# Four graph attention layers from packed neighbour lists: lists split by upper and lower half of the target rows

## The chip, the cores and the metric

The kernel runs on one core of one Trainium2 chip. The metric is the device time of one execution in microseconds (us). A core has TensorE (PE, with its weight loads shown as PEld), VectorE (DVE), ScalarE (ACT), GpSimd (POOL), SyncE (SP) and 16 DMA engines. The profile shows one execution.

## The reference

Four layers work on one graph of 4096 nodes with 256 features. Each is `x = layernorm(x + gat(x, adj))`. The adjacency has one entry in 256, plus the diagonal, and is the same in all layers. Layers 0 and 1 have four heads of 64 columns, layer 2 has two heads of 128, and layer 3 has one score with a positive and a negative softmax, each of 256 columns. Cut to what matters:

```
h = (x @ W.T).reshape(C, H, D).transpose(1, 0, 2)
e = alpha_src[:, :, None] + alpha_dst[:, None, :]
e = leaky_relu(e, 0.2); e = where(adj == 0, -inf, e)
out = einsum('hij,hjd->hid', softmax(e, axis=-1), h)
```

Layer 3 takes `softmax(e)` and `-softmax(-e)`, multiplies both by `x`, joins them, multiplies by `fc_W` and applies elu.

## The kernel before

**Tiles.** Target nodes are worked on in 32 row tiles of 128 (`P`). A row tile needs only the source nodes that touch any of its 128 targets, some 40% of them. So the kernel builds, once, a list for each row tile: the source nodes outside the tile that have an entry in it, packed into 13 tiles of 128 (`NG`), with an 8-bit mask of 128 targets for each listed node. The row tile's own 128 nodes are a fourteenth tile at position 6 (`FRONT`). All four layers use the same lists. Where a list doesn't fit its windows, a flag is set and `dense_layers` computes everything again at the end.

**Lists** (`Program.lists`). A block of four row tiles is read by `prepare`: 67 MB of adjacency in all arrive as int32, ACT turns them into bytes (L385) and DVE finds which source nodes touch which tile (L389). `places` (L394) ranks the hits with a few small matmuls and about nine DVE operations. `pack` (L427) then goes through the 31 other source blocks of a row tile: a DVE comparison makes a one-hot matrix of the places that this block can reach (L440, 128 to 384 columns by `WINDOW`), and one matmul for each reachable tile (L446, 73 for a row tile) moves mask bytes and the node number's digits to their place, 132 columns (`MC`). ACT copies three packed tiles at a time out of PSUM (L453), in five copies for a row tile, and DVE puts the digits together to the index list (L460 to L462). The packing banks come in turn from three PSUM banks (`pthree`).

**Order.** `run` computes layer 0's projections first, with the first ten packs and the `prepare` parts between them (`LEAD = 10`). Then it goes through layer 0's row tiles, and between the two halves of each of the first 22 it builds one more list. A scheduler orders the instructions of each engine from there; each engine works through its own queue in order.

**A row tile** (`RowTile`). It has two halves of seven positions (`HALF`). `load` (L632) loads the scores `S`, the masks `mk`, and one row of values for each listed node: a direct DMA on SP for the tile's own rows (L644) and an indirect one on POOL for each of the 13 other positions (L647). The first six of them reach only the first 17 blocks of nodes (`MIX`), so they can start before the layer before has stored the rest. The rows land in buffers `G` of two pools, `g0` with 16 and `g1` with 14, two positions in a buffer, in layer 3 one. `half` (L651) makes the weights `w`, 128 listed nodes by 128 targets for each position and head: in layers 0 and 1 ACT takes three heads' exponentials (L712) and DVE one head's product (L704, L708), then DVE masks two heads at a time (L681), after it has copied the masks to PSUM (L666). In layer 2 ACT does both heads and DVE masks each (L714); in layer 3 it is L690 to L694. TensorE multiplies them. In layers 0 and 1 the values are the stationary operand, 65 columns, and the weights stream (L724); the result stands transposed, so `copy` (L749) and `back` (L757) turn it round. In layers 2 and 3 the weights are stationary and the values stream, 129 and 257 columns (L727). `finish` normalises, adds the residual, and `norm` applies the layer norm to groups of tiles; `Projection` then makes the next layer's rows.

**Whole rows.** In layer 2 the blocks 3, 7 and 6, and in layer 3 the block 7, are not taken from lists: `whole_rows` goes over all 32 source blocks with four row tiles at a time (L1016 to L1027). These steps are spread between the list tiles (20 in layer 2, 28 in layer 3). At a layer's end `close` projects what is left and already loads and computes first halves of the next layer.


Of the kernel before, what the change touches and what calls it, by code (L numbers as in the profile page):

```python
# [50 lines left out]
P = 128  # L51
# [19 lines left out]
NG = 13  # L71
NP = NG + 1
CAP = NG * P
HALF = NP // 2

GROUPS = (((24, 4),), ((28, 2),), ((16, 2), (17, 1), (20, 2), (24, 1), (31, 2)), ((28, 1), (31, 4)))
LEAD = 10
MIX = 17
FRONT = 6
NODES = tuple(MIX * P if t < FRONT else N for t in range(NG))  # L80
MC = P + 4
# [11 lines left out]
KEXP = 10.0  # L93

# [11 lines left out]
def windows():  # L106

    share = 1.0 - (1.0 - 1.0 / 256.0) ** P
    mean, sd = P * share, (P * share * (1.0 - share)) ** 0.5
    dev = 4.5  # L110
    out = {}
    for m in range(NT):
        for j in range(NT):
            if j == m:
                continue
            if j < MIX:
                n = sum(q != m for q in range(j))
                lo = mean * n - dev * sd * n ** 0.5
                hi = mean * (n + 1) + dev * sd * (n + 1) ** 0.5
            else:  # L120
                n = sum(q != m for q in range(j, NT))
                lo = CAP - mean * n - dev * sd * n ** 0.5
                hi = CAP - mean * (n - 1) + dev * sd * (n - 1) ** 0.5
            a = max(0, int(lo // P))
            b = min(NG - 1, int((hi - 1) // P))
            out[m, j] = (a, b - a + 1)
    return out
# [3 lines left out]
assert all(a >= FRONT for (m, j), (a, _) in WINDOW.items() if j >= MIX)  # L131
WMAX = max(n for _, n in WINDOW.values()) * P
# [7 lines left out]
def kernel(ctx: ExitStack, tc: tile.TileContext, ins: dict, out: bass.AP):  # L140
# [14 lines left out]
        "maskC": dram.tile([NT, P, NP, MC], U8, name="maskC"),  # L155
# [38 lines left out]
class Program:  # L194


    def __init__(self, tc, ctx, ins, out, shared):
# [5 lines left out]
        self.g0 = self.pool("g0", 16)  # L203
# [89 lines left out]
    def lists(self, ctx):  # L293
# [21 lines left out]
        for k, sh in enumerate((8, 4, 0)):  # L315
# [21 lines left out]
        nc.gpsimd.affine_select(out=bt[:, :, :MIX], in_=bt[:, :, :MIX], pattern=[[NT, BT], [1, MIX]],  # L337
                                compare_op=ALU.is_gt, fill=0.0, base=0, channel_multiplier=-1)
        nc.vector.tensor_scalar(bt[:, :, MIX:], bt[:, :, MIX:], -1.0, None, op0=ALU.mult)

        nc.gpsimd.affine_select(out=bt[:, :, MIX:], in_=bt[:, :, MIX:], pattern=[[-NT, BT], [-1, NT - MIX]],
                                compare_op=ALU.is_ge, fill=0.0, base=-MIX, channel_multiplier=1)


        lo = cst.tile([P, NT, NT], F16, name="lo")
        wid = cst.tile([P, NT, NT], F16, name="wid")
        nc.gpsimd.memset(lo, 0.0)
        nc.gpsimd.memset(wid, 0.0)
        for j in range(NT):
            m = 0  # L350
            while m < NT:
                if m == j:
                    m += 1
                    continue
                e = m
                while e < NT and e != j and WINDOW[e, j] == WINDOW[m, j]:
                    e += 1
                a, n = WINDOW[m, j]
                nc.gpsimd.memset(lo[:, m:e, j], a * P - 1.0 - (CAP if j >= MIX else 0))
                nc.gpsimd.memset(wid[:, m:e, j], float(n * P))  # L360
                m = e
        limit = cst.tile([P, NP], F32, name="limit")
        nc.vector.memset(limit[:, :FRONT], float(MIX * P - 1))
        nc.vector.memset(limit[:, FRONT:], float(N - 1))
        total = cst.tile([P, NT], F32, name="total")
        bad = cst.tile([P, BT, NT], F32, name="bad")
        nc.vector.memset(bad, 0.0)

        class Block:
            def __init__(self, blk):  # L370
                self.blk = blk
                self.mk = mkp.tile([P, NT, BT, MC], U8, name="mk")
                self.red = wk.tile([P, BT, NT], F32, name="red")
# [53 lines left out]
            def pack(self, it):  # L427
# [4 lines left out]
                for j in order:  # L432
                    a, n = WINDOW[m, j]
                    for k in range(a, a + n):
                        touches.setdefault(k // 3, []).append((j, k))
# [1154 lines left out]
```

## Time and profile before

| | |
|---|---|
| three runs | 2753.11 us median (2740.87 to 2766.65) |
| span of the profiled execution, first to last instruction | 2249.3 us |
| mean granted TensorE clock in it | 0.966 |
| busy in the span | PE 2014.0, DVE 1786.6, ACT 1737.9, POOL 1494.4 us |
| gathers (L647) | 1456, mean 1017 ns busy |
| DMA | 493 MB, mean 219 GB/s |
| chain that ended last | PE 16% of the span, of it L727 12% and L1027 4% |

The profile gives no time for the profiled execution but its span; what lies around the span is seen only as the difference to the runs. In the profile's rows a group is named by its line, engine and operation, then output and inputs, then the count, busy time and mean duration. Starts are counted from the span's start. Busy time on PE is modelled, and matmuls overlap, so the distance between starts tells more than a duration. Layer 0's first half tile starts on PE at 168 us, layer 1 follows at about 810, layer 2 at 1340, and layer 3 at 1757.

### The profile page before, as it was taken

To read this page: it belongs to the slowest core of one execution; us is meant where nothing else is said; L and a number is where in the kernel's file an instruction comes from. 1 tells how busy PE (TensorE), PEld (TensorE's weight loads), DVE (VectorE), ACT (ScalarE), POOL (GpSimd) and SP (SyncE) were. 2 spreads that over 40 slices of the span, in tenths; PEclk is the share of its full clock that TensorE was granted. 3 is DMA by queue.
4 is the path that set the end of the run, shared out by engine and by line. 5 is a ranking of instruction groups with operands and counts; after the bars stand their busy time and mean duration, and the time that the engine had idled before them with its cause. 6 is when DMAs were issued, how large, how long until landed. Compare 5 with 4: busy or idle time off the path is not lost. (4 is left out here: it accounts for less than half of the span.)

```text
span 2249.3 us, 49137 instructions
## 1 busy us (share of the span) xinstructions
PE 2014.0 (90%) x15689; PEld 1834.3 (82%) x15689; DVE 1786.6 (79%) x5060; ACT 1737.9 (77%) x4989; POOL 1494.4 (66%) x1597
## 2 busy tenths in 40 slices
PE   4878889989999969988899898989999999999995
PEld 2658788878899859988888798989998888788784
DVE  2889899999999959987988886887876566566566
ACT  4778988988789859987888776987876677667664
POOL 2107655656677777777777777777773477777773
PEclk7999999999999989999999999999999999999998
DMA  8879877777566665666665666777777688888884
GB/s 284 258 245 360 272 219 250 254 247 228 146 170 191 174 202 168 182 175 175 173 185 162 172 167 171 226 209 223 223 227 225 200 282 280 249 284 270 262 248 130
DMA packets 250319, 492.99 MB, mean 219 GB/s; under 512 B 44385, under 2 KB 156610, under 8 KB 249666
## 3 DMA queue, kind: packets, MB, share of 16 engines
q0 software_dynamic: 81536, 245.30, 38.3%
q1 hardware_dynamic: 163906, 240.26, 33.3%
q10 hardware_dynamic: 4608, 4.20, 0.5%
q8 instruction: 126, 2.06, 0.4%
q14 instruction: 143, 1.17, 0.2%
HBM read 437.05 MB, written 52.54 MB: 218 GB/s over the span
## 5 line engine op out<-in xcount | busy, mean ns | idle before, releaser
L647 POOL DMA_INDIRECT G<-vals,idx x1456 | 1480.7, 1017 | 715.7 <-issue 221.1
L712 ACT ACTIVATE w<-S,G 128x128 f32<-128x128 f32 x3248 | 1001.6, 390 | 140.6 <-DMA G<-vals,idx 101.6
L724 PE MATMUL bank<-w,G 128*65 128x128 f32 x7168 | 837.8, 276 | 59.7 <-DVE w L681 59.3
L724 PEld LDWEIGHTS bank<-w,G 128*65 128x65 f32 x7168 | 798.7, 140 | 69.9 <-DVE w L681 68.4
L681 DVE SCALAR_TENSOR_TENSOR w<-w,bank 128x1792 f32<-128x1792 f32 x256 | 514.6, 2013 | 13.4 <-ACT w L712 11.2
L727 PE MATMUL bank<-G,w 128*128 128x257 f32 (+1 forms) x2660 | 490.8, 342 | 25.7 <-ACT z L1102 13.6
L727 PEld LDWEIGHTS bank<-G,w 128*128 128x128 f32 x2660 | 431.9, 195 | 73.2 <-ACT z L1102 16.4
L1027 PE MATMUL bank<-vw,pw 128*128 128x129 f32 (+1 forms) x2048 | 298.5, 301 | 3.7 <-issue 2.3
L1027 PEld LDWEIGHTS bank<-vw,pw 128*128 128x128 f32 x2048 | 273.6, 191 | 20.1 <-issue 2.8
L690 ACT ACTIVATE w<-S,G 128x128 f32<-128x128 f32 x385 | 137.8, 393 | 136.8 <-DMA G<-vals,idx 90.0
L440 DVE TENSOR_SCALAR oh<-iota,place 128x256 bf16<-128x256 f16 (+2 forms) x992 | 221.8, 298 | 9.4 <-PE bank L446 9.1
L704 DVE TENSOR_TENSOR w<-S,G 128x256 f32<-128x256 f32 x384 | 151.9, 416 | 69.9 <-DMA G<-vals,idx 66.5
L446 PE MATMUL bank<-mk,oh 128*128 128x132 fp8e4 x2336 | 192.1, 226 | 13.8 <-ACT cm L453 7.0
L557 PE MATMUL bank<-wext,xT 128*128 128x268 f32 (+3 forms) x640 | 176.9, 409 | 16.9 <-ACT xT L548 14.1
L446 PEld LDWEIGHTS <-oh 128*128 128x128 bf16 x2336 | 146.9, 99 | 50.4 <-DVE oh L440 12.7
L385 ACT ACTIVATE mk<-raw 128x1024 uint8<-128x1024 int32 x128 | 130.5, 1051 | 28.0 <-DMA raw<-in_adjB_dram 27.7
L557 PEld LDWEIGHTS bank<-wext,xT 128*128 128x128 f32 x640 | 117.2, 200 | 36.0 <-ACT xT L548 16.9
L1017 DVE SCALAR_TENSOR_TENSOR pw<-pw,mw 128x512 f32<-128x512 f32 x192 | 127.6, 689 | 18.2 <-ACT pw L1016 17.5
L1016 ACT ACTIVATE pw<-Sw,d 128x512 f32<-128x512 f32 x192 | 133.2, 711 | 7.5 <-PE bank L1027 7.0
L714 DVE SCALAR_TENSOR_TENSOR w<-w,mk 128x896 f32<-128x896 f32 x80 | 86.6, 1086 | 41.1 <-ACT w L712 37.9
L1024 DVE TENSOR_TENSOR pw<-pw,mw 128x512 f32<-128x512 f32 x64 | 43.6, 691 | 85.4 <-ACT pw L1023 48.0
L692 DVE TENSOR_TENSOR w<-w,mk 128x896 f32<-128x896 f32 x55 | 60.0, 1091 | 59.5 <-ACT w L691 58.2
(140 smaller groups left out, 1563.3 us busy)
## 6 DMA issues: line engine op xcount, KB each, us to landing
raw<-in_adjB_dram SPq DMA_DIRECT2D x128, 512.0 KB
mk<-maskC SPq DMA_DIRECT2D x112, 231.0 KB
G<-vals,idx POOLq DMA_INDIRECT x1456
S<-edge SPq DMA_DIRECT2D x64, 256.0 KB
vw<-vals SPq DMA_DIRECT2D x96, 129.0 KB
xp<-y SPq DMA_DIRECT2D x96, 128.0 KB
y<-xp SPq DMA_DIRECT2D x96, 128.0 KB
mw<-maskW SPq DMA_DIRECT2D x20, 528.0 KB
```

Of the source, the lines that this page charges most:

```text
L440: nc.vector.tensor_scalar(oh[:, :n * P], iota[:, :n * P], self.place[:, it, j:j + 1], None, op0=ALU.is_equal)
L446: nc.tensor.matmul(accs[b][:, s * MC:(s + 1) * MC], oh[:, (k - a) * P:(k - a + 1) * P], mk[:, j, it, :].bitcast(FP8), start=touches[b][0] ...
L557: nc.tensor.matmul(pp[:, :c1 - c0], self.xT[:, k, :], wext[:, k, c0:c1], start=(k == 0), stop=(k == KT - 1 and brow is None))
L647: nc.gpsimd.indirect_dma_start(out=self.place(pos), out_offset=None, in_=sh["v"][n][:NODES[t], :], in_offset=bass.IndirectOffsetOnAxis(ap= ...
L681: nc.vector.scalar_tensor_tensor(pair, pair, LEAST, mh2, op0=ALU.max, op1=ALU.mult)
L690: nc.scalar.activation(w[0][:, k, :], S[:, 0, :], AF.Relu, bias=d(k, 0))
L704: nc.vector.tensor_tensor(w[h][:, k:k + 2, :], S[:, h:h + 1, :].to_broadcast([P, 2, P]), dd[:, :, V + T + h:V + T + h + 1].to_broadcast([P ...
L712: nc.scalar.activation(w[h][:, k, :], S[:, h, :], AF.Exp, bias=d(k, h))
L724: nc.tensor.matmul(accs[0][:Wd, h * P:(h + 1) * P], v, w[h][:, k, :], **how)
L727: nc.tensor.matmul(a, w[h][:, k, :], v, **how)
L1016: nc.scalar.activation(p, S[:, h], AF.Exp, bias=d)
L1027: nc.tensor.matmul(accs[it][:, c:c + Wd], p[:, it, :], v[:, c:c + Wd], start=(j == 0 and h == heads[0]), stop=(j == NT - 1), skip_group_ch ...
```

## The change

The targets of a row tile are split into its upper and lower 64 rows. A source node that touches only one half of the rows is put into a list for that half, one that touches both is put into a mixed list. Five packed tiles hold the upper list and five the lower one; they are taken in pairs, and a pair shares one block of weights of 128 columns, the first 64 for the upper gather and the last 64 for the lower. Three mixed tiles hold the nodes that touch both halves and what the five-tile lists can't take. With the tile's own rows there are nine blocks of weights (`NU`) in place of fourteen, from the same thirteen indirect gathers and one direct load. The first half of a row tile has four blocks (its own, three pairs), the second five (two pairs, three mixed).

With it: `lists` ranks three classes, keeps one window for each class and source block, and writes the node's digits twice; `MIX` goes from 17 to 23; a buffer `G` holds seven positions (in layer 3 four), with four buffers in each of `g0` and `g1`; in all layers the weights are now the stationary operand, 64 columns wide for the members of a pair, with the output in the upper or lower 64 PSUM partitions; `copy` and `back` are gone. The core of the diff:

```diff
-NG = 13
-NP = NG + 1
-CAP = NG * P
-HALF = NP // 2
+HP = P // 2
+NPAIR = 5
+NMIX = 3
+NPACK = NPAIR + NMIX
+NU = NPACK + 1
+NP = 2 * NPAIR + NMIX
+HALF = 7
+FIRST = 3
+UNITS = (1 + FIRST, NPACK - FIRST)
+FULL = ((0,), tuple(range(NPAIR - FIRST, NPACK - FIRST)))
+PAIRS = (tuple(range(1, 1 + FIRST)), tuple(range(NPAIR - FIRST)))
...
-MIX = 17
-FRONT = 6
-NODES = tuple(MIX * P if t < FRONT else N for t in range(NG))
-MC = P + 4
+MIX = 23
+MC = P + 8
...
+PER = tuple(HALF if n < 3 else 4 for n in range(4))
+SLOT = max(p * r for p, r in zip(PER, ROW))
...
-        self.g0 = self.pool("g0", 16)
+        self.g0 = self.pool("g0", 4)
...
-        self.g1 = self.pool("g1", 14)
+        self.g1 = self.pool("g1", 4)
...
             def places(self):
...
+                cls = wk.tile([P, 3, BT, NT], BF16, name="cls")
+                nc.vector.tensor_scalar(cls[:, :2], self.red, 0.0, None, op0=ALU.is_gt)
...
+                nc.vector.tensor_tensor(flat[:, 2], flat[:, 0], flat[:, 1], op=ALU.mult)
+                nc.vector.tensor_tensor(flat[:, 1], flat[:, 1], flat[:, 2], op=ALU.subtract)
...
+                nc.vector.scalar_tensor_tensor(far, at[:, :2], float(NPAIR * P), cls[:, :2], op0=ALU.is_ge,
+                                               op1=ALU.mult)
...
+                nc.vector.tensor_tensor(place, place, here[:, 0], op=ALU.add)
+                nc.vector.tensor_tensor(place, place, here[:, 1], op=ALU.add)
...
             def pack(self, it):
...
-                    nc.vector.tensor_scalar(oh[:, :n * P], iota[:, :n * P], self.place[:, it, j:j + 1], None,
-                                            op0=ALU.is_equal)
-                    for k in range(a, a + n):
+                    nc.vector.tensor_scalar(oh[:, :len(ks) * P], iota[:, :len(ks) * P], self.place[:, it, j:j + 1],
+                                            None, op0=ALU.is_equal)
+                    for i, k in enumerate(ks):
...
-    def place(self, pos):
+    def slot(self, half, s):
         L, n = self.layer, self.layer.n
-        per = 1 if n == 3 else 2
-        s = pos // per
-        if s not in self.slots:
-            if n == 3:
-                other = self.step % 2 == 0 if self.step > 3 else self.step > 1 and s < HALF
-            else:
-                other = n > 0 and s * per >= HALF
-            pool = L.prog.g1 if other else L.prog.g0
-            self.slots[s] = pool.tile([P, 2 * ROW[0]], F32, name="G")
+        if (half, s) not in self.slots:
+            pool = L.prog.g1 if n > 0 and half else L.prog.g0
+            self.slots[half, s] = pool.tile([P, SLOT], F32, name="G")
+        return self.slots[half, s]
...
+            nc.sync.dma_start(out=self.place(0, 0), in_=sh["v"][n][m * P:(m + 1) * P, :])
...
+        for k in range(1 - half, HALF):
+            pos = half * HALF + k - 1
             nc.gpsimd.indirect_dma_start(
-                out=self.place(pos), out_offset=None, in_=sh["v"][n][:NODES[t], :],
+                out=self.place(half, k), out_offset=None, in_=sh["v"][n][:N if half else MIX * P, :],
                 in_offset=bass.IndirectOffsetOnAxis(ap=sh["idx"][:, m, pos:pos + 1], axis=0))
+    def parts(self, half):
+        out, k = {}, 0
+        for u in range(UNITS[half]):
+            if u in PAIRS[half]:
+                out[u] = [(slice(0, HP), self.place(half, k)), (slice(HP, P), self.place(half, k + 1))]
+                k += 2
+            else:
+                out[u] = [(slice(0, P), self.place(half, k))]
+                k += 1
+        return out
...
             for h in range(A):
-                for k in range(HALF):
-                    nc.scalar.activation(w[h][:, k, :], S[:, h, :], AF.Exp, bias=d(k, h))
+                for u in range(U):
+                    for rows, g in parts[u]:
+                        nc.scalar.activation(w[h][:, u, rows], S[:, h, rows], AF.Exp, bias=d(g, h))
...
-                if n < 2:
-                    nc.tensor.matmul(accs[0][:Wd, h * P:(h + 1) * P], v, w[h][:, k, :], **how)
-                else:
-                    a = accs[h][:, :Wd] if n == 3 else accs[0][:, h * Wd:(h + 1) * Wd]
-                    nc.tensor.matmul(a, w[h][:, k, :], v, **how)
+            turns = ((3, 0), (1, 2)) if n < 2 else ((0,), (1,))
+        for t, heads in enumerate(turns):
+            for us in (FULL[half], PAIRS[half])[::-1 if t == 1 and (half == 1 or n < 3) else 1]:
+                for h in heads:
+                    for u in us:
+                        for rows, g in parts[u]:
+                            a = accs[h][rows, :Wd] if n == 3 else accs[0][rows, h * Wd:(h + 1) * Wd]
+                            nc.tensor.matmul(a, w[h][:, u, rows], g[:, h * Wd:(h + 1) * Wd],
+                                             start=half == 0 and u == 0 and (n == 3 or h == turns[0][0]),
+                                             stop=half == 1, skip_group_check=True)
...
-        if part == 0 and m >= 1:
-            self.tile(m - 1).back()
```

## The prediction

> **What bounds the kernel now.** I read the page's totals first, then busy time by stretch, then POOL's timeline, its waits, and PE's timeline and chain. The totals say little, because every engine is near 80%:
>
> ```profile
> span 2249.3 us, 49137 instructions
> PE 2014.0 (90%) x15689; PEld 1834.3 (82%) x15689; DVE 1786.6 (79%) x5060; ACT 1737.9 (77%) x4989; POOL 1494.4 (66%) x1597
> ```
>
> Busy time by stretch separates the stages: start and first lists; layer 0 beside the lists (168 to 645); the rest of layer 0 and all of layer 1 (645 to 1313); layer 2 (1372 to 1690); its end; layer 3 (from 1760).
>
> ```profile
> 60.00:168.00 108.00, 87.89 (x878) 67.64 (x877) 94.57 (x417) 81.61 (x210) 10.08 (x10) 0.94 0.81 255
> 168.00:645.00 477.00, 429.50 (x4290) 393.77 (x4291) 459.96 (x1369) 412.50 (x1225) 303.57 (x299) 0.98 0.75 243
> 645.00:1313.00 668.00, 597.23 (x5057) 562.12 (x5056) 571.79 (x1307) 561.04 (x1899) 507.20 (x525) 0.97 0.64 178
> 1372.00:1690.00 318.00, 305.29 (x2504) 296.88 (x2503) 259.26 (x661) 265.88 (x726) 248.31 (x221) 0.99 0.75 217
> 1690.00:1760.00 70.00, 61.77 (x399) 55.09 (x398) 48.81 (x204) 39.42 (x105) 18.36 (x19) 0.98 0.70 212
> 1760.00:2220.00 460.00, 440.85 (x1987) 381.91 (x1987) 278.39 (x825) 308.81 (x649) 348.80 (x340) 0.98 0.84 261
> ```
>
> The columns are PE, weight loads, DVE, ACT, POOL, clock, DMA share, GB/s. From 168 to 645 DVE is busy 96% of the time: it sets the pace, 477 us for 22 tiles. From 645 to 1313 no column is full, but POOL's timeline shows that gathers cost more than their busy time:
>
> ```profile
> 1060.89 0.95 POOL L647 DMA_INDIRECT G<-vals,idx  x1 [0.30 <-ACT w L712]
> 1062.14 0.95 POOL L647 DMA_INDIRECT G<-vals,idx  x1 [0.30 <-DVE b L1073]
> ```
>
> One gather starts every 1.254 us, and the 0.30 us between them stands whoever is named as releaser. 525 gathers in this stretch are 658 of its 668 us: POOL is full. A tile has 13 gathers, so it cannot take less than 16.3 us. In layer 2 and after it POOL does wait, for PE to free buffers:
>
> ```profile
> POOL G L647 <- PE bank L727: 26.8, 22, 8.7
> ```
>
> (1313 to 1760: total, times, longest.) So PE paces layer 2 (18.3 us a tile), and nearly layer 3, where 340 gathers take 458 us, 1.35 each. PE's rows give the price of a matmul; every fp32 matmul stands in the trace as two records:
>
> ```profile
> 1006.74 6.28 PE L724 MATMUL bank<-w,G 128*65 128x128 f32 x56
> 1354.75 9.86 PE L1027 MATMUL bank<-vw,pw 128*128 128x129 f32 x86
> 1756.74 6.07 PE bank L727 x28
> 1390.76 0.95 PE L278 MATMUL bank<-ablk,nat 128*128 128x1 f32 x8
> ```
>
> A record with 128 moving columns takes 0.109 us, with 129 0.112, with 257 0.217; one moving column still takes 0.11, so that is the load of 128 weight columns, hidden behind wider matmuls.
>
> **What the change leaves alone.** A tile keeps 13 gathers (ten for pairs, three mixed) and its own direct row load, of the same bytes. Where POOL is full, 645 to 1313, I cost every edit at nothing: the half tiles get lighter on ACT, DVE and PE, but gathers hide them. If that cover were gone, DVE would be next, at 86% there.
>
> **Lists: dearer.** The one-hot op on L440 compares against 3.81 blocks of 128 on average instead of 2.35 (the windows of WINDOW counted). Its durations by width are:
>
> ```profile
> L440 DVE TENSOR_SCALAR oh<-iota,place 128x256 bf16<-128x256 f16 x123 | 30.7, 293 | 0.0
> L440 DVE TENSOR_SCALAR oh<-iota,place 128x384 bf16<-128x384 f16 x102 | 28.8, 313 | 0.0
> ```
>
> These run 0.20 and 0.23 us apart, so 0.03 us a block: 31 ops x 1.46 x 0.033 = +1.5 us of DVE a tile. `places` grows from nine to about thirty DVE ops per block of four tiles: thirteen on 256 elements at 0.335 us (the spacing of L704's 256-element ops), some ten on 128 at 0.2, the small ones 1.5 together: 8.2 against 1.4, so +6.8 us a block. Packing needs 118 matmuls instead of 73 a tile, 45 x 0.058 = +2.6 us of PE. Before layer 0's first tile lie ten packs and three `places`: 15 + 20 = 35 us more DVE in a stretch where DVE is busy 94.6 of 108. I take +34; if all idle time there took it up, +20; with stalls between packs, +45. The other 22 tiles and five `places` add 33 + 34 = 67 us.
>
> **Layer 0 and 1 half tiles: lighter.** L681 masks 1792 elements four times a tile in 2.01 us; L714 does 896 in 1.086, so 1.035 ns an element: 1024 cost 1.22 and 1280 1.48, and a tile falls from 8.05 to 5.40. L704 and L708 fall from 2.40 to 1.47, L666 by 0.17: together -3.75 us of DVE a tile, -82 over the 22 tiles beside lists. Against +67 that leaves -15; I take -12, bounds -35 and +15. On PE, weights and values change places: 112 records x 0.109 = 12.2 us a tile become 32 full ones of 0.112 (weight load) and 80 half-wide ones between 0.056 and 0.112. That, ACT's lighter exponentials and the dropped transposes (L749, L757) are worth nothing here, because DVE, then POOL, set the pace.
>
> **Layer 2: the main gain, if there is one.** 40 of a tile's 56 records become 64 columns wide and write partitions 0 to 63 or 64 to 127, alternating; the built program gives them column tiles of 128x64 at 0 and 64. Moving columns stay 129, so alone each still costs 0.112. No row of this trace shows two such matmuls at once: bounds are no overlap (0) and full overlap, 20 x 0.112 = 2.24 us a tile. I take full overlap, as weight loads already hide behind matmuls in L724's row. Tile modes change four times a tile. The nearest rows:
>
> ```profile
> 1012.85 1.05 PE L557 MATMUL bank<-wext,xT 128*128 128x262 f32 x4
> 1013.83 0.70 PE L560 MATMUL bank<-brow,ones 1*128 1x262 f32 x2
> 1014.46 0.46 PE L757 MATMUL bank<-ident,aT 65*128 65x65 f32 x4
> 1716.37 0.27 PE L589 MATMUL bank<-ident,row 128*1 128x128 f32 x1
> 1716.48 0.61 PE L727 MATMUL bank<-G,w 128*128 128x129 f32 x4
> ```
>
> L560, on a 32-row tile, costs 0.315 a record against 0.221, about 0.09 extra; L589, on a 32-column tile, starts the next matmul 0.11 later, no extra. So 0 to 0.1 a switch, at most 8 us in the layer; the column tile is nearer, I take 0.02. PE then falls from 18.3 to 16.1 us a tile, below POOL's 16.3 to 16.6. Twenty tiles x 1.8 = -36 and 2 for waits at the layer's end: -38, bounds 0 and -55.
>
> The Trainium skill, "TensorEngine Tiling (Array Packing)", Key Properties, says that tiles run in parallel but that changing the tiling mode drains TensorE. A drain, by the 0.276 us that a matmul lasts against its 0.11 spacing, would be 0.17 a switch: 14 us in layer 2 and 29 in layer 3. "TensorE: Matmul & The Clock Gate", Part 3, states 2.38 times for three column tiles; by that efficiency (2.38 of 3) a pair would run 1.6 times as fast, and the 44.8 us of PE that full overlap saves in layer 2 would be 33. L589's row speaks against the drain; the speed-up no row here shows.
>
> **Layer 3.** PE needs 56 x 0.217 = 12.2 us a tile plus 4.0 for the whole rows. With overlap it is 11.8, six switches add at most 0.6, and POOL takes over. But first halves (two slots of four positions) now live in four slots: only two tiles' fit where four did, so twelve gathers move past the point at which layer 2's last row is stored. In POOL's built order they stand between the second halves of tiles 0 and 1, waiting for PE. So 352 gathers x 1.27 = 447 instead of 458: -11, bounds +10 and -20. MIX at 23 makes those first halves wait for tile 22, next to last in layer 2's order; POOL's idle time from 1690 to 1760 covers it, and it costs 15 us (twelve gathers) if not.
>
> **Sum.** +34 - 12 - 38 - 11 = -27 us, a span of about 2222. The runs' median, 2753.1, lies 503.8 above the profiled span; the page shows nothing of that time, and I leave it unchanged: 2726. A run of this kernel tells about 1%, 27.5 us, from no change.
>
> **Rivals.**
> - *Column halves do not overlap.* Then PE stays the bound in layers 2 and 3, with the switches on top: +34 - 12 + 6 + 10 = +38, so 2791, slower. It decides where upper and lower 129-column records start 0.11 us apart, not 0.056 on average. For it: no row shows overlap. Against it: nothing but the separate column positions.
> - *The lists eat it all.* Overlap works, but three PSUM banks now serve one tile's pack until its last block (five were used in turn), so each next pack waits for its copy-out, about 1 us (L453 takes 0.5): 32 x 0.9 = +29, so about 2755, no change. For it: DVE has no slack there. Against: one-hot buffers and layer 0's own work fill such gaps.
> - *The lists overflow and the dense path runs.* Counted on the reference's own adjacency, the fullest tile needs 345 of the 384 mixed places, and none falls outside its window. I give it 0.01; the time would be far above all else.
>
> **How the numbers follow.** Forecast 0.49, no overlap 0.29, lists eat it 0.21, overflow 0.01. The forecast's own range, 2690 to 2755, straddles the 1% line: 0.33 faster, 0.16 same. The lists rival gives 0.03 faster, 0.14 same, 0.04 slower; no overlap 0.03 same, 0.26 slower; overflow 0.01 slower. Together faster 0.36, same 0.33, slower 0.31. The range takes in the second rival and most of the first: 2680 to 2812.
>
> **What would show it.** Right: layer 0's first half tile near 200 us instead of 168; tiles beside the lists still 21 us with DVE at 95%; 1.254 us a gather through layer 1; pairs of 129-column records in 0.11 us; layer 2 near 16.6 us a tile with POOL's waits on PE gone. Wrong: upper and lower starts 0.11 apart or more, tiles beside the lists well off 21 us, or gathers whose spacing changed.

## The result, and the profile after

The changed kernel took 2868.1 us (four runs, 2859.5 to 2869.4) against 2747.0 for the kernel before beside it (2737.6 to 2766.7): 1.042 times, 95% interval 1.038 to 1.047. That is slower, and above the range of the prediction. Its span is 2866.6 of 2868.3 us, so almost nothing lies around it.

Runs came in series, each on one chip, and the kernel before took about 2251 us in some of them ("quiet" below) and 2747 to 2796 in others ("slow"), so every ratio is taken within one series. The execution shown before the change was of the quiet kind, the times beside it and the result of the slow kind. In the one quiet series that had it, the changed kernel took 2324.5 against 2251.3 (1.033, 1.029 to 1.037).

First the totals of the changed kernel's page (result's run), with the row of the granted clock in 40 slices. Now no engine is near full, and the clock is low where the kernel before had nines:

```profile
span 2866.6 us, 50904 instructions
PE 2175.4 (76%) x16927; PEld 1760.2 (61%) x16927; DVE 1635.2 (57%) x5055; ACT 1537.9 (54%) x4857; POOL 1448.4 (51%) x1530
PEclk7987667677767765555555656779999989888887
```

Busy time by stretch, for the changed kernel in a quiet series: start, tiles beside lists, rest of layer 0 and layer 1, layer 2, layer 3 (PE, weight loads, DVE, ACT, POOL, clock, DMA share, GB/s):

```profile
60.00:217.00 157.00, 126.04 (x1384) 105.94 (x1382) 130.09 (x510) 82.82 (x197) 13.05 (x8) 0.84 0.65 210
217.00:732.00 515.00, 421.20 (x5159) 384.39 (x5159) 453.17 (x1437) 338.79 (x1116) 287.30 (x297) 0.79 0.64 201
732.00:1408.00 676.00, 548.29 (x5041) 465.40 (x5041) 442.71 (x1186) 487.33 (x1901) 507.34 (x529) 0.67 0.63 174
1460.00:1690.00 230.00, 208.06 (x1872) 195.22 (x1873) 180.65 (x504) 194.52 (x570) 179.68 (x166) 0.96 0.76 220
1900.00:2260.00 360.00, 298.51 (x1562) 191.50 (x1560) 196.57 (x656) 212.89 (x510) 275.92 (x277) 0.93 0.85 268
```

The clock is 0.79 and 0.67 in layers 0 and 1, where it was 0.98 and 0.97, and DVE, 96% busy beside the lists before, is down to 88% (453 of 515 us). Its waits in that stretch say for what: the one-hot comparisons of the lists (L497) need their buffers back from the packing matmuls on PE (L503), 41.3 us in 36 waits where the kernel before had 4.8 in two. PE itself waited 3.7 us for the packed tiles to be copied out (4.3 before), so the copy-out is not what holds it up (total, times, longest, us):

```profile
DVE oh L497 <- PE bank L503: 41.3, 36, 2.5
PE bank L503 <- ACT cm L509: 3.7, 1, 3.7
```

Busy time by stretch again, of the result's run and then of the kernel before in a slow series, without the start:

```profile
215.00:950.00 735.00, 527.56 (x5157) 458.39 (x5156) 469.33 (x1436) 338.73 (x1116) 284.41 (x298) 0.71 0.46 141
950.00:1780.00 830.00, 620.32 (x4766) 521.63 (x4767) 419.56 (x1110) 457.96 (x1789) 509.65 (x527) 0.59 0.50 139
...
2380.00:2800.00 420.00, 340.13 (x1604) 211.10 (x1600) 207.99 (x700) 222.97 (x529) 292.29 (x286) 0.87 0.79 239
```

```profile
171.00:819.00 648.00, 494.55 (x4274) 436.91 (x4274) 473.33 (x1359) 410.23 (x1213) 292.70 (x299) 0.87 0.56 179
819.00:1660.00 841.00, 678.39 (x4857) 605.01 (x4857) 556.18 (x1253) 540.09 (x1828) 503.99 (x525) 0.87 0.50 140
...
2250.00:2690.00 440.00, 388.22 (x1649) 322.94 (x1648) 243.04 (x728) 263.03 (x542) 303.83 (x294) 0.93 0.78 238
```

Milestones from four traces (before_look, after_third, before_x and the result's run) say in which stage the time went (us from the span's start; the last list is the copy of a tile's own block in its pack):

| | before, quiet | after, quiet | before, slow | after, slow |
|---|---|---|---|---|
| first half tile of layer 0 on PE | 167.3 | 217.3 | 171.5 | 214.5 |
| last list | 643 | 732 | 819 | 950 |
| layer 2's first gather | 1313.2 | 1408.8 | 1659.5 | 1781.9 |
| end of the span | 2248.9 | 2320.8 | 2749.5 | 2866.6 |

The differences, stage by stage: +50, +39, +7 and -24 in the quiet series, +43, +88, -9 and -5 in the slow one. The whole loss is made before the last list is packed.

### The profile page after: what moved, and what is told of

Its sections match the earlier page's. It is cut to its first block, busy times and chain, and to the rows that moved or that the text cites. A ratio compares the mean times of both kernels' runs of the same rounds, so it can differ in the third digit from the quotient of the medians.

```text
span 2866.6 us, 50904 instructions
## 1 busy us (share of the span) xinstructions
PE 2175.4 (76%) x16927; PEld 1760.2 (61%) x16927; DVE 1635.2 (57%) x5055; ACT 1537.9 (54%) x4857; POOL 1448.4 (51%) x1530
## 5 line engine op out<-in xcount | busy, mean ns | idle before, releaser
L812 PE MATMUL bank<-G,w 128*64 128x65 f32 (+5 forms) x9828 | 1200.0, 334 | 375.4 <-issue 287.9
L812 PEld LDWEIGHTS bank<-G,w 128*64 128x64 f32 (+1 forms) x9828 | 965.5, 211 | 625.3 <-issue 431.3
L798 ACT ACTIVATE w<-S,G 128x64 f32<-128x64 f32 (+1 forms) x3248 | 861.0, 351 | 79.9 <-DMA G<-vals,idx 42.1
L497 DVE TENSOR_SCALAR oh<-iota,place 128x640 bf16<-128x640 f16 (+3 forms) x992 | 300.7, 352 | 246.6 <-PE bank L503 130.7
L1093 PE MATMUL bank<-vw,pw 128*128 128x129 f32 (+1 forms) x2048 | 344.3, 320 | 68.3 <-issue 67.2
L503 PE MATMUL bank<-mk,oh 128*128 128x136 fp8e4 x3782 | 331.5, 253 | 79.3 <-issue 63.3
L756 DVE SCALAR_TENSOR_TENSOR w<-w,bank 128x1024 f32<-128x1024 f32 (+1 forms) x256 | 344.4, 1346 | 50.5 <-ACT w L798 39.7
L503 PEld LDWEIGHTS <-oh 128*128 128x128 bf16 x3782 | 292.7, 114 | 111.2 <-issue 79.4
L623 PE MATMUL bank<-wext,xT 128*128 128x268 f32 (+3 forms) x640 | 229.4, 502 | 35.8 <-ACT xT L614 20.6
L766 ACT ACTIVATE w<-S,G 128x64 f32<-128x64 f32 (+1 forms) x385 | 128.6, 357 | 189.6 <-DMA G<-vals,idx 138.0
L794 DVE TENSOR_TENSOR w<-S,G 128x384 f32<-128x384 f32 (+1 forms) x192 | 95.7, 507 | 31.1 <-DMA G<-vals,idx 24.4
```

The lines of the kernel that those rows point to most:

```text
L497: nc.vector.tensor_scalar(oh[:, :len(ks) * P], iota[:, :len(ks) * P], self.place[:, it, j:j + 1], None, op0=ALU.is_equal)
L503: nc.tensor.matmul(accs[b][:, s * MC:(s + 1) * MC], oh[:, i * P:(i + 1) * P], mk[:, j, it, :].bitcast(FP8), start=touches[b][0] == (j, k), ...
L623: nc.tensor.matmul(pp[:, :c1 - c0], self.xT[:, k, :], wext[:, k, c0:c1], start=(k == 0), stop=(k == KT - 1 and brow is None))
L756: nc.vector.scalar_tensor_tensor(pair, pair, LEAST, mh2, op0=ALU.max, op1=ALU.mult)
L766: nc.scalar.activation(w[0][:, u, rows], S[:, 0, rows], AF.Relu, bias=d(g, 0))
L798: nc.scalar.activation(w[h][:, u, rows], S[:, h, rows], AF.Exp, bias=d(g, h))
```

## The experiments

**Where the 503.8 us lie.** The kernel before, unchanged:

> The kernel before once more, unchanged, to see an execution like the timed ones. Theory S (the 503.8 us that I put around the span do not lie there; the execution shown of before ran in a state that its timed runs were not in): span within 5 us of its time, so 2735 to 2765, granted clock well below the 0.966 shown, 0.70 to 0.88, more than 500 stretches of over 0.6 us in which PE starts nothing (117 in the shown one), and gathers no longer 1.254 us apart on end through layer 1. Rival O (the time does lie around the span): span near 2249, clock 0.97, time 2740 to 2765. Under S my price list for the tiles was read in a state that does not hold.

It took 2252.3 us with a span of 2250.6, at a clock of 0.96: both texts were wrong about the time, since this series was a quiet one. The time lies inside the span, and the shown execution and the shown times came from series of different kinds. It was traced again beside later runs; before_look fell in a quiet series (2251.3 us, span 2248.9), before_x in a slow one (2757.1, span 2749.5 of 2751.3):

> The kernel before once more, for its trace beside the others of this series. In one series it took 2251 us at a clock of 0.964, in another 2796 at 0.89, where the changed kernel's trace holds some 800 stretches of over 0.6 us, most of them multiples of 0.70, in which PE starts nothing and waits for nothing (102 in the run with full-width pairs of the other series). Theory B (in the slower series PE's issue is stopped in steps of 0.70 us, for any kernel): at about 2250 some 117 such stretches, at about 2750 to 2800 over 500. Rival: at 2750 and above the stretches stay near 117 and the time is lost on DMA or POOL.

> The kernel before, for its trace in a series where it takes about 2790 (it was traced at 2251 so far). In such a series all nine traces of the changed kernel and its variants hold some 500 to 600 stretches of 0.70, 1.40 or 2.10 us in which PE starts nothing and waits for nothing, almost all after the first 200 us; in the quiet series 18 to 36. Theory B (the slower series halt PE in such steps, whatever the kernel): 400 to 600 of them here too, layer 0 beside the lists and layer 2 both longer than the 21.5 and 18.4 us a tile of the quiet series. Rival: fewer than 100, and the time is lost on another engine. If the series is a quiet one: 2245 to 2260, 18 such stretches.

Theory B held, at the edge of its 400 to 600. PE's starts in the kernel before, slow series (start, duration, instruction, and the idle time before it):

```profile
1103.30 6.10 PE L724 MATMUL bank<-w,G 128*65 128x128 f32 x48
1109.60 0.27 PE L724 MATMUL bank<-w,G 128*65 128x128 f32 x1 [0.19 <-issue]
1110.32 0.27 PE L724 MATMUL bank<-w,G 128*65 128x128 f32 x1 [0.46 <-issue]
1111.05 0.31 PE L724 MATMUL bank<-w,G 128*65 128x128 f32 x1 [0.46 <-issue]
1111.75 0.27 PE L724 MATMUL bank<-w,G 128*65 128x128 f32 x1 [0.39 <-issue]
```

After 48 records in a row, single ones start 0.72, 0.73 and 0.70 us apart, and "issue" says that they waited for nothing the profile shows. Counted over matmuls and weight loads, to within 0.05 us, there are 396 distances of 0.70, 1.40 or 2.10 us in this trace and 15 in the quiet one; the changed kernel has 535 in the result's run and 22 in a quiet one. The 396 add up to 333 of the 501 us by which this trace is longer than the quiet one. In every slow trace nearly all of them come after the first 200 us. DVE and ACT, too, idle there with nothing to wait for that the profile shows (82 and 70 times, against 0 and 1 in the quiet trace). One chip gave a quiet series and, some 22 minutes later, a slow one, so it is not the chip alone; what halts PE stays open.

**Are column tiles the cost?** Every paired matmul at full width, here and in the last half of layer 3:

```diff
 for rows, g in parts[u]:
+    rows = slice(0, P)
     a = accs[h][rows, :Wd] if n == 3 else accs[0][rows, h * Wd:(h + 1) * Wd]
```

> The changed kernel with every paired matmul at full width: all 128 weight columns into all 128 rows, the same number of matmuls, no column tiles and no changes of tile shape; it leaves out that the two members of a pair go to different rows. Theory C (column tiles are what costs: their switches and the two matmuls at once slow PE or its clock): 2700 to 2780, clock above 0.80. Rival L (the lists and what they make wait are the cost, and column tiles at least help): 2860 to 2950, since PE then has 20 x 0.1 us more a tile in layers 2 and 3 and 80 x 0.05 in layers 0 and 1. Rival G (less work on DVE and ACT leaves PE waiting more, whatever its tile shape): within 1% of 2868.

Its series was a quiet one. The four runs took 2506.5 to 2574.7 us against 2250.7; the ratio, 1.118 (1.112 to 1.124), is that of the two fastest and already far above the changed kernel's 1.033. So column tiles, taken together, are no cost; theory C is out. The trace shows what hurts. PE's timeline of this run, at 782 and at 1094 us:

```profile
782.15 3.29 PE L813 MATMUL bank<-G,w 128*128 128x65 f32 x28
...
1094.60 30.71 PE L813 MATMUL bank<-G,w 128*128 128x65 f32 x143
```

Less the last one's own duration, the first row is 0.112 us from start to start, the second 0.213, the same instructions back to back. Busy time by stretch of the same run, two stretches of layer 1:

```profile
1070.00:1270.00 200.00, 186.98 (x845) 181.18 (x846) 78.71 (x184) 89.75 (x344) 111.13 (x117) 0.50 0.40 114
1300.00:1570.00 270.00, 269.63 (x2247) 256.19 (x2246) 191.57 (x487) 212.66 (x835) 205.55 (x212) 1.00 0.62 177
```

In the first the clock stays at 0.50 for 200 us although PE is 93% busy, in the second, with the same work, at 1.00 for 270 us; layers 2 and 3, with 129 and 257 columns over the same load, have it at 0.97 on average (1650 to 2500 us). From there came theory K. The same kernel and the changed one, and the one test that alters only what is streamed:

> The changed kernel, unchanged, beside the kernel before on this chip. With full-width matmuls it was 1.118 times the kernel before, at a granted clock of 0.84 to 0.87; in its windows layers 0 and 1 ran at 0.64 to 0.83, although PE was busy 94 to 99% of them. Theory K (with the weights stationary a matmul of layers 0 and 1 streams only 65 columns over a load of 128, and the clock is granted by what is streamed, so it falls to half): still slower than before, 1.04 to 1.11, clock below 0.90, low in layers 0 and 1 and near 1 in layers 2 and 3, where 129 and 257 columns are streamed. Rival D (only column tiles bring trouble: full-width ones were slow for want of overlap): 0.97 to 1.01.

> The changed kernel, unchanged, for its ratio in this series. If the kernel before takes about 2250 here: theory K (the clock, which falls where 65 columns are streamed over a load of 128) expects 1.05 to 1.12, the 1.118 of full-width pairs less what overlap saves; if it takes 2750 to 2800, 1.04 to 1.05 as twice before.

> The changed kernel, but every matmul of a half tile in layers 0 and 1 streams 130 columns (two heads' values) instead of 65, so twice the streaming for the same loads; it leaves out that each head's columns hold that head's sum alone. Theory K (the clock goes by what is streamed): clock in layers 0 and 1 rises above 0.85, and the time stays within 1% of the changed kernel or falls below it, although PE is given more to do. Rival W (PE is bound by its work, and the clock is an effect of something else): 40 couples more of 0.05 us and 12 full ones of 0 to 0.1 each half tile's worth, so 2 to 4 us a tile more, 64 tiles: 100 to 250 us slower than the changed kernel, clock unchanged.

```diff
-nc.tensor.matmul(a, w[h][:, u, rows], g[:, h * Wd:(h + 1) * Wd],
+v = g[:, h * Wd:(h + 1) * Wd]
+if n < 2:
+    a, v = accs[0][rows, h * Wd:(h + 2) * Wd], g[:, :2 * Wd]
+nc.tensor.matmul(a, w[h][:, u, rows], v,
```

The run after_third was the quiet one of the first section; its 1.033 lies below K's 1.05 to 1.12. The other two were slow. The changed kernel took 2923.2 against 2796.0, 1.045 (1.040 to 1.049), clock 0.74; with twice the columns 2859.1, 1.021 (1.017 to 1.026), clock 0.84. More streaming for the same loads took 2.2% away, so K holds and W is out. Beside the lists the clock rose from 0.70 to 0.83 (K had asked for 0.85), and that stretch took 685 us, against 747 in the changed kernel and 648 in the kernel before (its slow trace). It came out so twice more: 1.025 (1.023 to 1.027), and

> The changed kernel with 130 columns streamed instead of 65 in layers 0 and 1 (each head's columns then do not hold that head's sum alone), for a quiet series. Theory K: the last list 15 to 40 us earlier than the 732 us of the changed kernel, a clock beside the lists above its 0.73 to 0.86, 1.012 to 1.03 of before. Rival W (PE is bound by its work): later than 732 us, 1.05 to 1.09. In a series with the kernel before near 2750 to 2800: 1.02 to 1.025.

at 1.017 (1.013 to 1.021), again in slow series; the last list came at 885 to 904 us in the three, not at 950 and 965. In a quiet series it never ran. From 220 to 860 us, first this run and then the result's:

```profile
220.00:860.00 640.00, 475.01 (x4890) 399.27 (x4892) 442.39 (x1379) 332.69 (x1099) 282.34 (x280) 0.83 0.51 156
```

```profile
220.00:860.00 640.00, 458.00 (x4425) 397.76 (x4422) 412.22 (x1257) 302.69 (x979) 243.24 (x255) 0.70 0.48 147
```

In equal time 4890 matmuls started instead of 4425, at a clock of 0.83 instead of 0.70.

**Values stationary again.** In layers 0 and 1 the old operands with the new lists, with `copy` and `back` put back:

```diff
+if n < 2:
+    nc.tensor.matmul(accs[0][:Wd, h * P + rows.start:h * P + rows.stop], v, w[h][:, u, rows], **how)
+    continue
```

> The new lists and half tiles, but in layers 0 and 1 the values are stationary again and 128 weight columns are streamed, as before the change, with the copy and the transposes back; for a pair both members are multiplied over all 128 columns, so it leaves out that they go to different rows. Theory K: the loss goes away but for the lists' own price: 1.00 to 1.03 times before, clock above 0.93, gathers 1.254 apart through layer 1. Rival L (the lists themselves are what costs, in waits between packs): stays above 1.06, first half of the run slow at a full clock.

> As the run with values stationary, but a pair's members stream only their own 64 columns, which is the whole computation. Theory K: 80 of 104 records of a tile stream 64 columns over a load of 65, so the clock falls again in layers 0 and 1, below 0.85, and the time lies 2 to 8% above that of the run with 128 columns, although it streams less. Rival W (PE's work is the bound): 80 x 0.05 = 4 us of PE a tile less, equal to or below the run with 128 columns.

Both in the slow series with before at 2796: 1.012 (1.008 to 1.016) and 1.011 (1.006 to 1.015). Most of the loss is gone, as K says, though the clock of 0.93 was not reached (0.875 with 128 columns; the kernel before had 0.89 in that kind of series). That 64 columns would again cost 2 to 8% was wrong. The spacings by clock say why: a record of 64 columns over a load of 65 takes 0.059 us at full clock and 0.110 at half, one of 128 over 65 takes 0.109 and 0.213, one of 65 over 128 takes 0.112 and 0.213. So what counts is how much of the time is filled with streaming, not how many columns a record has. Both runs also take the column tiles, and with them the changes of tile shape, out of layers 0 and 1, so of these experiments only the doubled columns isolate the streaming.

That can be counted. In all traces the clock changes only at multiples of 3.41 us. For each such stretch I added up what its matmuls stream at full clock (0.844 ns a column for fp32, from 257 in 0.217 us; 0.434 for the packing, from 136 in 0.059; half of it for a column half), and looked at the clock of the next stretch. Six quiet traces together:

| streamed, share of the stretch | clock now 1.0: next at 1.0 | clock now 0.5: next at 1.0 |
|---|---|---|
| under 30% | 0 of 193 | 0 of 414 |
| 30 to 40% | 41 of 126 | 40 of 156 |
| 40 to 45% | 64 of 71 | 71 of 82 |
| over 45% | 2839 of 2842 | 171 of 171 |

The next clock follows the share, whatever the clock is now, with the edge near 38%. An edge there tells 81 of the 4055 stretches wrong; the best edge in PE's busy time, as the profile models it, tells 470 wrong, so being busy is not what counts. This explains each form. Back to back, 65 columns over a load of 128 stream 49% of the time at full clock, and 26% at half: it keeps whichever clock it has, so one pause, or one stretch of loads, drops it and it doesn't come back until denser work comes along. (The four runs at full width lie from 2506.5 to 2574.7, the traced one the slowest of them; no other kernel here spreads so far, as one expects of two stable paces.) The old form (128 over 65) streams 99%, and 51% at half: it climbs out in one stretch. So do 64 over 65 (92% and 49%) and 130 over 128 (98% and 51%). In the changed kernel only 32 of a tile's 112 records are of the weak form, 65 over 128 at full width. Its column halves are not: a couple takes 0.058 us at full clock and 0.108 at half (95% and 51%). What pulls the share down beside them are the full-width records, the changes of shape (0.205 us from full to half width, 0.348 at half clock) and the waits.

> Values stationary in layers 0 and 1, 64 columns streamed for a pair's member, the whole computation, beside the kernel before once more. In a series with before near 2250, theory K (the changed kernel's loss beside the lists is the clock, which falls where 65 columns are streamed over a load of 128) expects 2260 to 2280, 1.004 to 1.013 of before: the tiles beside the lists in 465 us as in the run with full-width pairs in layers 2 and 3, and the later start of 47 us against 20 to 27 gained in layers 2 and 3. Rival R (with column tiles in layers 2 and 3 the early stages are slow too): 1.03 as the changed kernel.

Again a slow series: 1.014 (1.011 to 1.017), so neither text could be tested, and the quiet figure is an estimate only (below).

**Column tiles in layers 2 and 3, and the packing,** both upon the run with 64 columns streamed:

> The run with values stationary and 64 columns streamed (1.0105), and in layers 2 and 3 every paired matmul at full width too, so no column tile is left in the half tiles; it leaves out there that the two members of a pair go to different rows. Theory H (column halves overlap and save PE time, as forecast: 2 us a tile in layer 2, 4 in layer 3): 2 to 5% slower than that run in layers 2 and 3, so 1.03 to 1.06 of before. Rival T (column tiles bring nothing there, because something else sets the pace or the overlap stalls): 0.99 to 1.015.

> The run with values stationary and 64 columns streamed for a pair's member (1.0105 times before, in a series with before at 2796), with the packing of the lists cut to 62 matmuls and 31 one-hot operations of two blocks a tile, less than the 73 and 2.35 of before; it leaves out most of the lists, so what is gathered is not what is wanted. Theory P (the lists' packing is what is left of the loss): the tiles beside the lists fall from 30 us to 26 or less and the time to 0.96 to 0.99 of before. Rival Q (the places, the slots, the order): within 1% of 1.0105, the tiles beside the lists near 30 us.

```diff
-return list(range(a, a + n)) + list(range(NPAIR + e, NPAIR + e + x))
+return [a + (n - 1) // 2, NPAIR + (e if j < 28 else e + x - 1 - j % 2)]
```

This series was quiet. Without column tiles (the edit of the full-width run, in these layers alone) 1.017 (1.015 to 1.020). Beside the lists, values stationary:

```profile
211.00:683.00 472.00, 407.03 (x5302) 377.88 (x5303) 453.32 (x1448) 356.32 (x1174) 296.85 (x295) 0.95 0.70 220
```

DVE is 96% busy again, at a clock of 0.95, and the stretch takes 472 us: 4 less than before the change, 43 less than the changed kernel's 515. The comparisons' waits for the packing matmuls are back to what they were:

```profile
DVE oh L497 <- PE bank L503: 4.5, 6, 1.6
```

From layer 2's first gather to the end it takes 933.5 us, against 912.0 with column tiles and 935.7 before: so the tiles are worth 21.5 us in layers 2 and 3, between H and T. Nearly all of it lies in layer 2: from its first gather to its last half-tile matmul on PE 413.9 us without them and 394.7 with them. Together, values stationary in layers 0 and 1 and column tiles in 2 and 3 would give about 2290.7 - 21.5 = 2269 in a quiet series, an estimate, still not below 2251.

With the packing cut to 62 matmuls the first half tile comes at 192.4 us instead of 211.0, the last list at 650 instead of 683, and layer 2's first gather at 1329.4 instead of 1355.0. From there to the end, however, it takes 943.3 us with its false lists, against the 912.0 above, and beside the lists its clock is 0.90. So the time, 1.008 (1.005 to 1.010), misses P's 0.96 to 0.99 and lies within Q's 1%, and the run does not price the packing by itself. The milestones show that the packing is a part of what is left; that the `places` and their chain are the other part is not shown.

> The run with values stationary and 64 columns streamed, with six lists instead of ten made ahead of layer 0's first tile, and windows of 4.0 instead of 4.5 standard deviations (117 blocks for 122). Theory P (the later start is packing work on PE and DVE ahead of the first tile, in a stretch where both have some 20% to spare): layer 0's first tile 30 to 45 us earlier, the tiles beside the lists 20 to 30 us longer in the whole as there are four more, the time 10 to 25 us below that run, 0.995 to 1.003 of before. Rival V (DVE's sum sets it, wherever it lies): within 0.3% of that run.

```diff
-LEAD = 10
+LEAD = 6
-    dev = 4.5
+    dev = 4.0
```

This one was slow again: 1.015 (1.011 to 1.018), within 0.2% of the run it is built on. The first tile came 41 us earlier (173.0 against 214.2), and the last list 92 us later: the work only moved, as rival V says.

**Layer 2 without its masking operations:**

```diff
-if n == 2:
-    nc.vector.scalar_tensor_tensor(w[h], w[h], LEAST, mh, op0=ALU.max, op1=ALU.mult)
-elif h % 2 == 0:
+if n < 2 and h % 2 == 0:
...
-nc.vector.scalar_tensor_tensor(p, p, LEAST, mj, op0=ALU.max, op1=ALU.mult)
```

> The changed kernel without the two masking operations of layer 2 (scalar_tensor_tensor on DVE, for gathered blocks and for whole rows); the mask is left out of that layer. In layer 2 of the changed kernel POOL idles only 9.6 of 230 us beyond the 0.30 between gathers, and a gather that lies over one of these operations lasts 0.22 to 0.29 us longer than the others. Theory M (these operations hold up the gathers, so POOL is full at 17.9 us a tile, not at 16.3): gathers of layer 2 back to 0.95, 16.3 to 16.8 us a tile, some 20 to 30 us less in the whole. Rival E (PE with its shape switches sets the pace of layer 2): 17.5 to 18 us a tile, time unchanged within 0.5%.

> The changed kernel without the masking operations of layer 2 (the mask is left out there). Where PE was halted in steps of 0.70 us, the gathers of layer 2 fell from 1.03 to 0.95 us, as theory M says (the masking operations hold up POOL's gathers), but the tiles took 24.6 us as PE set the pace. In a quiet series M expects 16.3 to 16.8 us a tile in layer 2 instead of 17.9, the whole 20 to 35 us below the changed kernel: 1.017 to 1.025 of before. Rival E (PE with its shape switches sets the pace of layer 2): 17.5 to 18 us a tile, 1.03. In a series that halts PE: 1.045 to 1.055, as before.

All three series with this kernel were slow (1.051, 1.048 and 1.047), and its layer 2 took 23.2 to 23.6 us a tile there (22.5 in the result's run), with POOL waiting for other engines between its gathers, so the time that M promised could not be seen. The mechanism could. POOL's gathers in layer 2, result's run, then without the masks (count, busy us, mean ns, idle):

```profile
L707 POOL DMA_INDIRECT G<-vals,idx x177 | 180.1, 1017 | 120.9 <-issue 52.9 <-ACT xT L614 16.0 <-ACT pw L1082 12.7
```

```profile
L707 POOL DMA_INDIRECT G<-vals,idx x172 | 163.5, 951 | 136.6 <-issue 50.9 <-PE bank L810 27.6 <-ACT erow L662 25.5
```

The mean falls from 1017 to 951 ns, to what a gather takes in layer 1. What the masks cost in time stays open, since no quiet series had this kernel.

## Why the prediction was wrong

**The time around the span.** The step "the page shows nothing of that time, and I leave it unchanged" failed. The 503.8 us are inside the span of a slow execution. It set the base right by luck (before was again 2747), but the shares that I costed came from a machine in another condition: in slow series layer 1 takes 20.2 to 20.7 us a tile in both kernels, where PE halts and POOL's gathers no longer follow one another.

**Tiles beside the lists: -12 forecast, +39 and +88 measured. This is the step that failed.** The sum itself, DVE +67 for lists and -82 for half tiles, was nearly right: with values stationary, at a clock of 0.95, the stretch came out 4 us shorter, with DVE at 96%. What failed is the sentence before it: on PE, "weights and values change places", "worth nothing here, because DVE, then POOL, set the pace". I priced the new records with 0.112 us, a row measured at full clock, as if the clock were given. With 65 columns streamed over 128 loaded it fell to 0.79 and 0.71 on average (quiet, slow). At half clock such a record takes 0.213 us, and the other work on PE pays as well, the lists' own packing too: 0.113 instead of 0.059 for a packing matmul. In the quiet trace 350 of the 680 full-width records beside the lists and 290 of the 2588 packing matmuls started at half clock, in the result's run 479 of 676 and 1159 of 2588. So PE made DVE wait (41.3 us in the quiet trace against 4.8 before, nearly the stage's whole loss), and DVE no longer set the pace alone. The Trainium skill's "TensorE: Matmul & The Clock Gate", Part 1, says that the clock is gated to half by a monitor of how busy PE was in windows of 3.4 us; the records here do change in multiples of 3.41 us, but PE was 93% busy at 0.50: loads did not count, only streaming did, from about 38% of a stretch on.

**The start: +34 forecast, +50 and +43 measured,** above and just under the bound of 45. The direction was right and packing is one cause (cutting it brought 19 us back), but the size was short. I put packing on DVE alone, 15 us, while its 45 more matmuls a tile also load a PE that was 81% busy there; that this is what was missing is not shown. (The parts that I gave for `places` add up to 7.9 us, not to 8.2, which is 2 us over eight blocks.)

**Layer 1: nothing forecast, and nothing came** (+7 and -9). In the quiet series this is for the reason given, the cover was POOL: its gathers stand 1.25 us apart, at a PE clock of 0.67:

```profile
1060.08 0.95 POOL L707 DMA_INDIRECT G<-vals,idx  x1 [0.30 <-issue]
1061.33 0.95 POOL L707 DMA_INDIRECT G<-vals,idx  x1 [0.30 <-issue]
```

**Layers 2 and 3: -49 forecast, -24 and -5 measured.** Overlap works: the first rival is out. Upper and lower records start 0.007 us apart, and a couple takes 0.110 us. In layer 2, quiet series, one busy row shows it (shape 128*64; count, busy us, mean ns):

```profile
L812 PE MATMUL bank<-G,w 128*64 128x129 f32 x472 | 32.3, 283 | 0.0
```

472 records one after another would be 52.9 us at 0.112. What failed is the floor that I set under it, "below POOL's 16.3 to 16.6". I took 1.254 us for a gather from layer 1. In layer 2 they are longer; the kernel before and the changed one, quiet series:

```profile
L647 POOL DMA_INDIRECT G<-vals,idx x160 | 180.2, 1126 | 48.8 <-issue 27.4 <-DMA G<-vals,idx 4.9 <-ACT w L712 3.7
```

```profile
L707 POOL DMA_INDIRECT G<-vals,idx x166 | 179.9, 1084 | 50.6 <-issue 45.4 <-ACT pw L1082 1.2 <-ACT w L798 0.9
```

The idle time is 0.305 us a gather, no more than in layer 1: POOL was full in this part of layer 2 before the change, too. The 26.8 us of waits for PE from which I read PE's pace lie almost all behind it, 23.2 of them from 1600 us on. 13 x (1.126 + 0.305) = 18.6 us a tile is the pace that I had put down to PE, and 13 x (1.084 + 0.305) = 18.1 after. So the 2 us saved on PE could be used only where POOL is not full.

In sum layer 2 still came near its term, and it was layer 3 that went the other way (quiet series). From layer 2's first gather to its last half-tile matmul on PE it took 429.4 us before and 394.7 after, -35 against the -38 forecast, of which column tiles are 19 (413.9 without them). From there to the end it took 506.3 before and 517.3 after, +11 where I had -11. I had counted twelve of layer 3's gathers as moved past that point; it was 22 (342 before, 364 after). POOL's pace there fell only from 17.3 to 17.1 us a tile, and did so without column tiles too (17.2).

**Switches of tile shape** were priced at 0.02 us, "the column tile is nearer". They cost 0.09: from a full to a half record 0.205 us at 129 columns and 0.310 at 257, against 0.112 and 0.217 without a switch. L560's row was the right neighbour. The drain of 0.17 that I worked out beside the rule of the Trainium skill's "TensorEngine Tiling (Array Packing)", Key Properties, was too dear, but the rule was right that a switch costs something and my reading of L589 was not.

**The second rival,** that the lists eat the gain, has the right place, but it gave 29 us where the stage missed its forecast by 51 and 100, and stalls for PSUM banks are not what the trace shows (3.7 us of waits for the copy-out, 4.3 before); it was the clock. Of the signs that I named, the first half tile near 200 us (217), 21 us beside the lists (23.4) and layer 2 near 16.6 (18.1) failed; 1.254 us a gather through layer 1 (in the quiet series) and couples in 0.11 us (0.110) held.

## What to carry to other kernels

A matmul's price includes the clock that it earns: before swapping operands, work out which share of the time streams columns, at full and at half clock (here a form that streams under 38% at half clock stays there), and charge the loss to every other PE instruction of the stage. An engine costed at nothing because another sets the pace needs a price for the case that its own rate halves. A price taken from one stage holds for that stage: the row of the same instruction in the stage that changes was there to be read.

## What the runs showed of the hardware

- The clock of each 3.41 us followed what was streamed in the one before, with an edge near 38%; weight loads did not hold it up. A form between (49% at full, 26% at half clock) has two stable paces.
- In some series PE halts in steps of 0.70 us, for the kernel before (396 times) and the changed one (535), and the same programs take 22 to 26% longer; quiet traces show 15 to 33 such distances. The cause is open.
- Gathers on POOL last longer while DVE runs a `scalar_tensor_tensor` in layer 2: in the changed kernel's quiet trace (1460 to 1690 us) the 51 that lie over neither masking operation for more than 0.2 us last 0.949 us on average, the other 115 last 1.143. The Trainium skill, "SBUF — State Buffer", section "Who interferes with whom", says that a DVE instruction with two SBUF inputs contends with a GpSimd instruction that reads SBUF; the runs without the masks (951 against 1017 ns) agree.
- Two fp32 matmuls on column halves do run at once: 0.110 us a couple at 129 columns, and at half clock 0.108 for a couple of 65 columns, against 0.213 for one full-width record.
